# Relative-position products that hold a 64×48 corner of the array for each head, in place of 128×48

## The chip, the cores and the metric

The kernel runs on one core of one Trainium2 chip. The metric is the device time of one execution, in microseconds (us). Three runs of the kernel before gave 2831.45, 2834.18 and 2834.56 us, a median of 2834.18. Cores work with five engines: TensorE (PE in the profile) multiplies matrices, and its weight loads have a row of their own (PEld); VectorE is DVE, ScalarE is ACT, GpSimd is POOL, and SyncE (SP) issues most DMAs.

## The reference

Two layers run on an image of 48 × 48 positions (2304 tokens) with 768 channels. The first is a transformer block with 12 heads of 64 channels, and the second a block of Fourier transforms and small matrix products. The change lies in the attention of the first:

```python
attn = jnp.einsum('bqc,bkc->bqk', q * scale, k)
coords = jnp.arange(H)[:, None] - jnp.arange(H)[None, :] + (H - 1)
Rh = rel_pos_h[coords]
Rw = rel_pos_w[coords]
r_q = q.reshape(B * nh, H, W, hd)
rel_h = jnp.einsum('bhwc,hkc->bhwk', r_q, Rh)
rel_w = jnp.einsum('bhwc,wkc->bhwk', r_q, Rw)
attn = (attn.reshape(B * nh, H, W, H, W) + rel_h[:, :, :, :, None] + rel_w[:, :, :, None, :]).reshape(B * nh, H * W, H * W)
attn = jax.nn.softmax(attn, axis=-1)
out = jnp.einsum('bqk,bkc->bqc', attn, v)
```

For every query at row h and column w, `rel_h` is its product with 48 vectors that depend on h, and `rel_w` with 48 vectors that depend on w. Both are small products: 64 channels, 48 vectors, and the 48 queries that share an h or a w.

## The kernel before

**Heads.** Channels lie on partitions. Two heads make a pair: `qT` holds head 0 on partitions 0 to 63 and head 1 on 64 to 127, for all 2304 tokens. `pr` counts the six pairs. A chunk `c` is G = 384 queries, eight image rows; each pair has six.

**A chunk.** For each of 18 key tiles `kt`, `scores` (L684) makes scores of both heads in one PSUM tile `sp`. `content` (L670) multiplies 64 channels of keys with 64 of queries, one head on each half of the rows of the array. `position` (L679) adds the relative terms in a single fp32r instruction per head, from `terms` and a constant `select`. ACT takes the exponential (L689) into `main`. Then come 18 `products` with the values (L702), in six groups of three key tiles; each product contracts over 128 keys and gives 64 channels, head 0 on PSUM partitions 0 to 63 and head 1 on 64 to 127. DVE sums the exponentials for the denominators (L833).

**The relative products.** `relT` (L213) has partitions, head j, direction (0 for h, 1 for w), and 112 vectors. For j = 0 the vectors are on partitions 0 to 63 and zeros on 64 to 127; for j = 1 the other way about (`constants`, L319). So one matmul with all 128 partitions of `qT` gives the products of one head alone. `relative(pr, c)` (L288, matmul L296) makes eight rows of `rel_h`, and `columns(pr, i)` (L264, matmul L272) eight columns of `rel_w`. Each is a batch of 8 × 2 matmuls into one PSUM bank, head j at partition 64 j. The moving operand has 48 columns. For `pr` = 0, `columns` reads `qT` and writes PSUM with strides; later pairs read `by_column`, a copy in order that ACT makes (L694). Each fp32 matmul is two instructions in the profile, each with its weight load, so a batch shows 32 matmuls. After a batch, `two_parts` (L233) copies the bank twice on ACT (L240, L241) and subtracts on DVE (L242); DMAs then spread the rows into `terms`.

**The order.** The order of PE's work is the order of the code: the attention runs under a manual schedule for PE and SP, and in its loop for ACT and DVE as well. `between` (L785) hangs the small work before the six groups of products. In chunks 0 to 2 of a pair, `relative` for three chunks later goes ahead of group 0. In chunk 3 of all but the last pair, three `columns` for the next pair go ahead of groups 0, 1 and 2; in chunk 4 again three, and a `relative` ahead of group 3; in chunk 5 a `relative` ahead of groups 0 and 2. Group 0 follows the scores directly, the others follow products. Nine batches of pair 0 run earlier, in the last third of the query, key and value projections (L642 to L648), whose matmuls (L529, L561) use 128 rows and 128 columns of the array. `inverses` (L731) puts a 128×48 matmul with 32 moving columns ahead of group 4 of each chunk.

After the attention come the projection (L918), the MLP (L1291, L1351, L1355) and the second layer (L1383 to L1639).

Of the kernel before, what the change touches and what calls it, by code (L numbers as in the profile page):

```python
# [20 lines left out]
HW = 48  # L21
# [25 lines left out]
def block_then_afno(  # L47
# [147 lines left out]
    with ExitStack() as flag_scope:  # L195
# [12 lines left out]
        with ExitStack() as att:  # L208
# [4 lines left out]
            relT = cst.tile([P, 2, 2, 112], F32, name="relT")  # L213
# [13 lines left out]
            def small_bank():  # L227
                banks.append(banks.pop(0))
                return banks[-1]
# [3 lines left out]
            def two_parts(hi, lo, src):  # L233

                both = shared[:, ds(3 * T + (copies[0] % 2) * G, G)]
                copies[0] += 1
                dims = {f"x{i}": k for i, k in enumerate(src.shape[1:])}
                names = " ".join(dims)
                both = both.rearrange(f"p ({names}) -> p {names}", **dims)
                nc.scalar.copy(both, src)  # L240
                nc.scalar.copy(hi, src)  # L241
                nc.vector.tensor_tensor(lo, both, hi.bitcast(F32), ALU.subtract)  # L242
# [19 lines left out]
            by_column = None  # L262

            def columns(pr, i):  # L264

                qT = heads[pr][0].rearrange("p (c b h w) -> p b w c h", c=6, b=3, h=8)
                bank = small_bank()
                ps = bank.rearrange("p (w c h) -> p w c h", w=8, h=8)
                for r in range(8):
                    w = 8 * i + r  # L270
                    for j in range(2):
                        nc.tensor.matmul(  # L272
                            bank[ds(64 * j, HW), ts(r, HW)] if pr else ps[ds(64 * j, HW), r],
                            relT[:, j, 1, 47 - w : 95 - w],
                            by_column[:, w] if pr else qT[:, w // 16, w % 16],
                            start=True, stop=True,
                        )
                hi, lo = (
                    a.rearrange("p (c b h w) -> p b w c h", c=6, b=3, h=8)[
                        :, i // 2, ds(8 * (i % 2), 8)  # L280
                    ]
                    for a in (col_hi, col_lo)
                )
                two_parts(hi, lo, ps)
# [3 lines left out]
            def relative(pr, c):  # L288

                qT = heads[pr][0][:, ts(c, G)].rearrange("p (b h w) -> p h b w", b=3, h=8)  # L290
                hp = small_bank()
                ps = hp.rearrange("p (b h w) -> p h b w", b=3, h=8)
                for r in range(8):
                    h = 8 * c + r
                    for j in range(2):
                        nc.tensor.matmul(  # L296
                            ps[ds(64 * j, HW), r], relT[:, j, 0, 47 - h : 95 - h], qT[:, r],
                            start=True, stop=True,
                        )
                row_hi = r_pool.tile([P, G], F32R, name="row_hi")  # L300
                row_lo = r_pool.tile([P, G], F32R, name="row_lo")
                two_parts(row_hi, row_lo, hp)
                terms = b_pool.tile([P, 3, 3, G], F32R, name="terms")
                ready[pr, c] = terms
                for j in range(2):
                    for n, (row, column) in enumerate(((row_hi, col_hi), (row_lo, col_lo))):
                        for i in range(3):
                            rows = ds(64 * j + 16 * i, 16)
                            nc.sync.dma_start(
                                out=terms[ds(64 * j + 16 * n, 16), i].bitcast(F32),  # L310
                                in_=row[rows].bitcast(F32).unsqueeze(1).to_broadcast([16, 3, G]),
                            )
                            nc.sync.dma_start(
                                out=terms[ds(64 * j + 32 + 16 * n, 16), :, i].bitcast(F32),
                                in_=column[rows, ts(c, G)].bitcast(F32)
                                .unsqueeze(1).to_broadcast([16, 3, G]),
                            )
# [12 lines left out]
            def queries_keys_values(qkv):  # L330
# [263 lines left out]
                for p in range(T // TB):  # L594
# [13 lines left out]
                    for n, (kind, i) in enumerate(orders[p]):  # L608
# [33 lines left out]
                        if p == 2 and n == 0:  # L642
                            fetch(0)
                        elif p == 2 and n in (1, 2, 3):
                            for j in (0, 1):
                                columns(0, 2 * (n - 1) + j)
                        elif p == 2 and n in (4, 6, 8):
                            relative(0, n // 2 - 2)  # L648
                        elif p == 2 and n == 5:
                            fetch_values(0)  # L650
                    part_by_part.close()

            with tc.manual_schedule(engines={mybir.EngineType.PE, mybir.EngineType.SP}):
# [8 lines left out]
                by_column = o_pool.tile([P, HW, HW], F32, name="by_column", bufs=1)  # L662
# [122 lines left out]
                def between(pr, c, acc):  # L785

                    last = pr == NC - 1
                    work = {
                        1: [partial(denominators, pr, c, acc)],
                        4: [partial(inverses, pr, c)],  # L790
                        5: [partial(left_apart, pr, c), stored],
                    }
                    if last and c > 2:
                        work[5] += [partial(spread_out, 0), partial(scaled, 1), stored]
                    else:
                        work[5] += [partial(spread_out, 1), partial(scaled, 1)]
                    if c < 3:
                        work[0] = [partial(relative, pr, c + 3)]
                    elif not last and c < 5:
                        for n in range(3):  # L800
                            work.setdefault(n, []).append(partial(columns, pr + 1, 3 * (c - 3) + n))
                        if c == 4:
                            work[3] = [partial(relative, pr + 1, 0)]
                    elif not last:
                        work[0] = [partial(relative, pr + 1, 1)]
                        work[2] = [partial(relative, pr + 1, 2)]
                    if not last and c in (2, 3):
                        for n in range(3):
                            i = 3 * (c - 2) + n
                            work.setdefault(n + (1, 3)[c - 2], []).append(  # L810
                                partial(in_columns, pr + 1, i)
                            )
                    return work
# [192 lines left out]
        with tc.If(safe < 1):  # L1006
            with ExitStack() as att:
# [18 lines left out]
                relT = cst.tile([HD, 2, 112], F32, name="g_relT")  # L1026
# [8 lines left out]
                for pr in range(NC):  # L1035
                    w3 = []
                    for n, name in enumerate(("g_wq", "g_wk", "g_wv")):
                        w = w_pool.tile([P, NC, P], F32, name=name)
# [36 lines left out]
                    for sg in range(T // SG):  # L1075
# [20 lines left out]
                        for i in range(2):  # L1096
                            hp = psum.tile([P, G], F32, name="g_hp", tag="m")
                            for r in range(8):
                                h = sg * 16 + i * 8 + r
# [13 lines left out]
                        for i in range(2):  # L1113
                            wp = psum.tile([P, 24, 16], F32, name="g_wp", tag="m")
                            for r in range(24):
                                w = i * 24 + r
# [712 lines left out]
```

## Time and profile before

| what | value |
|---|---|
| median of three runs | 2834.18 us |
| the profiled execution, its own time | 2834.65 us |
| its span, first to last instruction | 2832.9 us |
| mean granted TensorE clock | 0.996 of full |
| from first scores to start of the last chunk | 403.06 to 1388.31 us |
| matmuls at L272, by array shape | 1152 of 128×48 |
| matmuls at L296, by array shape | 1152 of 128×48 |
| matmuls at L670 and L679, by array shape | 2592 and 1296 of 64×128 |
| matmuls at L702, by array shape | 2592 of 128×64 |

How to read it: a line of a group names the line of code, the engine, the operation, what it writes and reads, then the rows × columns of the array that a matmul holds ("128*48"), the shape and type of what moves, and the count. Behind the bar are busy time in us, the mean duration of one in ns, and the idle time ahead of it. A line of the timeline begins with its start and its length in us; consecutive instructions of one kind are merged, with their count. A matmul's duration is a latency with a modelled end, and matmuls overlap; the distance from start to start tells how fast they follow each other.

### The profile page before, as it was taken

The numbers are of one execution on the slowest core, as the hardware profiler recorded it, in microseconds if no ns is written. First come the engines' busy times: TensorE is split into PE (matmuls) and PEld (weight loads), VectorE is DVE, ScalarE is ACT, GpSimd is POOL, SyncE is SP. The second block draws the span as 40 slices with busy tenths as digits, with TensorE's granted clock in tenths as the row PEclk, the third lists the DMA queues.
The fourth block names the chain that finished last, engine by engine and source line by source line (L and its number), as shares of the span: only waits on it lengthen the run. The fifth ranks groups of instructions, "written<-read, shape, count | busy, mean of one in ns | idle before, by whom it ended". The sixth has DMA issues, their size and how long they took to land. (4 is left out here: it accounts for less than half of the span.)

```text
span 2832.9 us, 41042 instructions
## 1 busy us (share of the span) xinstructions
PE 2788.5 (98%) x15759; PEld 1716.2 (61%) x15759; DVE 1700.6 (60%) x2520; ACT 920.6 (32%) x1466; POOL 668.7 (24%) x662
## 2 busy tenths in 40 slices
PE   8999999999999999999999999999999999999998
PEld 4555655656656565665555555555555555556887
DVE  5434236767676767676756756565565566566665
ACT  1101135656566565665401201131101201102332
POOL 2505010000000000000164233342242422222432
PEclk9999999999999999999999999999999999999999
DMA  4535375273664737455332112131121212123254
GB/s 149 182 103 162 106 158 111 58 133 69 105 126 65 132 64 133 85 82 99 110 132 79 53 65 67 45 101 56 45 67 62 95 45 67 45 70 108 62 162 142
DMA packets 218430, 269.09 MB, mean 95 GB/s; under 512 B 24645, under 2 KB 197053, under 8 KB 216689
## 3 DMA queue, kind: packets, MB, share of 16 engines
q1 hardware_dynamic: 215720, 264.33, 37.5%
q8 instruction: 127, 2.08, 0.3%
q10 hardware_dynamic: 2440, 1.84, 0.2%
q14 instruction: 79, 0.64, 0.1%
q0 software_dynamic: 64, 0.20, 0.0%
HBM read 150.25 MB, written 52.32 MB: 72 GB/s over the span
## 5 line engine op out<-in xcount | busy, mean ns | idle before, releaser
L689 ACT ACTIVATE main<-sp 128x768 f32<-128x768 f32 x648 | 516.3, 812 | 34.5 <-PE sp L679 19.6
L833 DVE TENSOR_TENSOR pairs<-pairs,main 128x1536 f32<-128x1536 f32 x252 | 443.0, 1758 | 27.1 <-DVE pairs L833 0.9
L679 PE MATMUL sp<-terms,select 64*128 64x384 f32 x1296 | 412.0, 629 | 0.0
L1353 DVE TENSOR_TENSOR main<-o,main 128x384 f32<-128x384 f32 x540 | 298.7, 556 | 39.3 <-PE o L1351 1.2
L1291 PE MATMUL h<-shared,w 128*128 128x384 f32 x864 | 296.6, 486 | 0.7 <-POOL w2s L167 0.7
L670 PE MATMUL sp<-shared 64*128 64x384 f32 x1296 | 265.2, 485 | 1.6 <-ACT row_hi L241 1.0
L670 PE MATMUL sp<-qT,kT 64*128 64x384 f32 x1296 | 264.1, 484 | 0.0
L1291 PEld LDWEIGHTS h<-shared,w 128*128 128x128 f32 x864 | 163.9, 190 | 116.1 <-POOL w2s L167 1.3
L735 POOL TENSOR_TENSOR inverse<-inverse,rden 24x32 f32<-24x32 f32 x36 | 15.1, 421 | 926.5 <-DVE sums L734 887.5
L1291 PE MATMUL h<-shared,w1s 128*128 128x384 f32 x648 | 226.6, 486 | 0.0
L1297 ACT ACTIVATE hT<-c,vec 128x384 f32<-128x384 f32 x108 | 66.5, 615 | 465.1 <-DVE c L1303 465.0
L702 PE MATMUL op<-main,shared 128*64 128x384 f32 x1296 | 217.4, 488 | 0.0
L702 PE MATMUL op<-main,v 128*64 128x384 f32 x1296 | 216.4, 488 | 0.0
L833 DVE TENSOR_TENSOR pairs<-main 128x1536 f32<-128x1536 f32 x36 | 63.3, 1758 | 248.1 <-ACT main L689 248.1
L1303 DVE TENSOR_TENSOR c<-h,u 128x384 f32<-128x384 f32 x108 | 60.1, 557 | 212.4 <-PE h L1291 212.4
L1351 PE MATMUL o<-w,hT 128*128 128x384 f32 x432 | 174.8, 487 | 2.4 <-DVE mv L125 2.0
L1351 PE MATMUL o<-w2s,hs 128*128 128x384 f32 x432 | 174.9, 487 | 1.6 <-DVE hs L162 1.6
L679 PEld LDWEIGHTS sp<-terms,select 64*128 64x128 f32 x1296 | 125.3, 186 | 83.7
L1291 PEld LDWEIGHTS h<-shared,w1s 128*128 128x128 f32 x648 | 123.1, 190 | 85.8
L167 POOL TENSOR_TENSOR w2s<-w 128x384 f32<-128x384 f32 x36 | 35.9, 998 | 566.0 <-DMA w<-in_mlp_w_dram 424.0
L529 PE MATMUL m<-main 128*128 128x384 f32 x504 | 164.6, 488 | 2.4 <-DVE main L179 1.8
L702 PEld LDWEIGHTS op<-main,v 128*64 128x64 f32 x1296 | 96.9, 137 | 92.7 <-issue 67.7
(209 smaller groups left out, 4136.6 us busy)
## 6 DMA issues: line engine op xcount, KB each, us to landing
w<-in_mlp_w_dram SPq DMA_DIRECT2D x72, 768.0 KB
terms<-col_parts SPq DMA_DIRECT2D x432, 72.0 KB
terms<-row_hi SPq DMA_DIRECT2D x216, 72.0 KB
terms<-row_lo SPq DMA_DIRECT2D x216, 72.0 KB
main<-in_qkv_w_dram SPq DMA_DIRECT2D x36, 384.0 KB
z<-zt SPq DMA_DIRECT2D x48, 192.0 KB
x<-in_x_blocks_dram SPq DMA_DIRECT2D x18, 384.0 KB
k_d<-o SPq DMA_DIRECT2D x36, 192.0 KB
```

Source lines behind the costliest of these rows:

```text
L167: eng.tensor_tensor(t[0], b12, b11, ALU.subtract)
L529: nc.tensor.matmul(bank, a[:, c, :], b[:, c, :], start=(first and c == 0), stop=(c == 2), skip_group_check=not first,)
L670: nc.tensor.matmul(sp[:, j, :G], kT[at, ts(kt, P)], qT[at, ts(c, G)], start=first, stop=not first,)
L679: nc.tensor.matmul(sp[:, j, :G], select[at, a % 2], ready[pr, c][at, a // 2, b], start=first, stop=not first,)
L689: nc.scalar.activation(p, sp[:, :, :G], AF.Exp, scale=HD**-0.5)
L702: nc.tensor.matmul(op[ts(j, 64)], v[:, kt, ts(j, 64)], exps[:, kt, j, :], start=(kt == 0), stop=(kt == NT - 1),)
L833: nc.vector.tensor_tensor(pairs, so_far, exps[:, ds(kt - 1, 2)], ALU.add)
L1291: nc.tensor.matmul(bank[i], a[:, c, :], b[:, c, :], start=(start and c == 0), stop=(c == 2), skip_group_check=not start,)
L1297: nc.scalar.activation(h[:, i, ts(k, G)], src, AF.Gelu, bias=col(V_B1 + 2 * n + i))
L1303: nc.vector.tensor_tensor(t, src, other, ALU.add)
L1351: nc.tensor.matmul(bank[k], a, b, start=start, stop=True, skip_group_check=not start)
L1353: nc.vector.tensor_tensor(dst, bank[k], dst, ALU.add)
```

## The change

Both the stationary and the moving operand of the two small matmuls are cut to the 64 partitions of their head. Head 0 then reads partitions 0 to 63 and writes PSUM partitions 0 to 63; head 1 reads and writes 64 to 127. The counts of instructions, the 48 moving columns, PSUM banks, order, copies and DMAs are as before. The zeros in `relT` stay and are not read.

```diff
@@ columns
                         nc.tensor.matmul(
                             bank[ds(64 * j, HW), ts(r, HW)] if pr else ps[ds(64 * j, HW), r],
-                            relT[:, j, 1, 47 - w : 95 - w],
-                            by_column[:, w] if pr else qT[:, w // 16, w % 16],
+                            relT[ts(j, 64), j, 1, 47 - w : 95 - w],
+                            (by_column[:, w] if pr else qT[:, w // 16, w % 16])[ts(j, 64)],
                             start=True, stop=True,
                         )
@@ relative
                         nc.tensor.matmul(
-                            ps[ds(64 * j, HW), r], relT[:, j, 0, 47 - h : 95 - h], qT[:, r],
+                            ps[ds(64 * j, HW), r], relT[ts(j, 64), j, 0, 47 - h : 95 - h],
+                            qT[ts(j, 64), r],
                             start=True, stop=True,
                         )
```

## The prediction

> **What bounds the kernel now.** I read the page first, then the groups of TensorE instructions, then stretches of the timeline around the changed matmuls.
>
> ```profile
> span 2832.9 us, 41042 instructions
> PE 2788.5 (98%) x15759; PEld 1716.2 (61%) x15759; DVE 1700.6 (60%) x2520; ACT 920.6 (32%) x1466; POOL 668.7 (24%) x662
> ```
>
> TensorE (PE) is busy for 98% of the span. A modelled busy time alone proves little, so I asked for the busy time by stretch. The attention lies between the first scores and the start of the last chunk:
>
> ```profile
> 403.06:1388.31 985.25, 984.63 (x8386) 591.50 (x8386) 660.62 (x557) 606.34 (x821) 56.52 (x69) 1.00 0.53 97
> ```
>
> The columns are span, then PE, PEld, DVE, ACT and POOL. PE leaves 0.6 us of 985 empty, at full clock; ACT and DVE are busy for about two thirds. Whatever lengthens or shortens PE's own sequence here moves the end by as much. The groups of PE that matter:
>
> ```profile
> L670 PE MATMUL sp<-qT,kT 64*128 64x384 f32 x1296 | 264.1, 484 | 0.0
> ...
> L702 PE MATMUL op<-main,v 128*64 128x384 f32 x1296 | 216.4, 488 | 0.0
> ...
> L272 PE MATMUL small<-by_column,relT 128*48 128x48 f32 x960 | 27.0, 209 | 0.0
> ...
> L296 PE MATMUL small<-qT,relT 128*48 128x48 f32 x576 | 16.4, 210 | 0.0
> ```
>
> "128*48" is the part of the array that an instruction holds: rows, then columns. An fp32 matmul appears twice, so a batch of 8 positions and 2 heads has 32 instructions. There are 72 batches (36 at L272, 36 at L296). Scores run at 64*128, the products with the values at 128*64, and the changed matmuls at 128*48. Means are no help (209 ns is a pipelined latency); spacing of starts is. In the timeline (start, duration, ...), a batch between two groups of products:
>
> ```profile
> 503.91 0.49 PE L702 MATMUL op<-main,shared 128*64 128x384 f32 x2
> 504.24 0.89 PE L272 MATMUL small<-by_column,relT 128*48 128x48 f32 x32
> 504.95 0.83 PE L702 MATMUL op<-main,shared 128*64 128x384 f32 x4
> ```
>
> A pair of products (one per head) normally repeats after 0.322 us, and here the batch follows after 0.33: no seam. The batch takes 0.71 us, 16 pairs at 45 ns; the single starts (the trace's records, to the ns) show the two heads of a pair 7 ns apart. So both heads already run side by side. 384 columns in 322 ns make 0.84 ns a column, 40 ns for 48: the pair is within 5 ns of one stream's time. Now the same batch inside 128*128 work (first line: one instruction of 0.322 us), and the seam from scores to products where no batch lies:
>
> ```profile
> 343.83 0.49 PE L529 MATMUL m<-main 128*128 128x384 f32 x1
> 344.24 0.93 PE L296 MATMUL small<-shared,relT 128*48 128x48 f32 x32
> 345.10 0.59 PE L529 MATMUL m<-main 128*128 128x384 f32 x1
> ```
>
> ```profile
> 1348.26 0.63 PE L679 MATMUL sp<-terms,select 64*128 64x384 f32 x2
> 1348.73 0.81 PE L670 MATMUL sp<-qT,kT 64*128 64x384 f32 x4
> 1349.08 0.63 PE L679 MATMUL sp<-terms,select 64*128 64x384 f32 x2
> 1349.64 0.87 PE L702 MATMUL op<-main,v 128*64 128x384 f32 x4
> ```
>
> 343.83 to 344.24 is 0.415 by the single starts (343.829, 344.244), 93 ns more than the 322 the instruction needs. L679 to the next L670 is 0.47; L679 to L702 is 0.56, again about 95 ns more. Every place in this trace where the shape changes has this gap, and none where it stays. Behind the gap the first weight load is uncovered too: the first two pairs of L702 there start 0.373 apart, not 0.322 (1349.643, 1350.016).
>
> **What the Trainium skill says.** "TensorEngine Tiling (Array Packing)", Key Properties: changing the tiling mode, not only the tile, drains the TensorE; 128×64 and 64×64 are different modes. The trace agrees for the changes it has, 93 to 97 ns each (the sums use 94), and shows that 48 columns count with 64. "TensorE: Matmul & The Clock Gate", Part 3 (The mechanism): a weight load overlaps matmuls in flight only when the row groups differ. That would favour the change, but the trace does not agree: the loads at L272 (125 ns each) are spaced like their matmuls, and share all rows. "PSUM — Partial Sum Buffer", PSUM bank collisions: by one quoted statement different row tiles cannot access the same bank at once, while what was measured there is a collision within one bank and 32-partition quarter. The changed pair shares a bank but not partitions; no row of before shows such a pair, since scores put each head in its own bank.
>
> **The change, part by part.**
>
> *Instructions.* None is added or removed: 2304 here, each with 48 moving columns. No DMA, copy or semaphore moves. What SBUF reads is halved, but spacing is set by columns: 64-row scores need 322 ns a pair, 128-row products also 322. I take zero for the spacing. Bounds: down to 40 ns, gaining 5 ns on 1008 attention pairs, 5.0 us; up to serial heads, +40 ns a pair (rival D).
>
> *Mode seams.* A batch goes from 128*48 to 64*48. In the attention it no longer has the products' mode. The other 9 batches, six at L272 and three at L296, lie in the projection stage. Of the 63 in the attention, 33 follow directly on scores and 30 on products; all 63 are followed by products. Counting: c 0 to 2 have one batch each (18, after scores); c 3 has three (one after scores), c 4 four (one), c 5 two (one), for five head pairs.
> - After scores: the entry was a change (64×128 to 128×64) and stays one (64×128 to 64×64): 0. Its exit becomes one: 63 exits in all.
> - After products: the entry becomes one: 30.
> - The 9 early batches: before and after are 128×128 work (one meets the scores), a change on both sides then and now: 0.
>
> 93 new changes. An exit costs 94 ns plus the weight load no longer covered: first to second pair of products 0.373 after a change, 0.339 behind a batch now (502.284, 502.623), so 34; 128 ns. An entry costs 94 plus 80 against 43 ns from first to second small pair (501.528, 501.608; 504.235, 504.278), 37; 131 ns.
> 63 × 0.128 + 30 × 0.131 = 8.1 + 3.9 = **12.0 us**.
>
> What is not shown: a change of the row split alone (128×64 to 64×64), which all 93 are. Bounds: 0, if only column splits drain, and 131 ns. I take the full price, because the skill names the mode as a whole and because 64×128 to 128×64, changing both, costs 95, the same as a column change alone: one drain, not a sum. Below nothing is excluded, as the seam now has no gap.
>
> *What hides it.* Nothing: PE has no slack in this stretch. Behind each seam wait only PE's own next matmuls, then the copies at L240 and L241, whose terms are used three chunks later or, for columns, a chunk later. ACT and DVE get some room; neither sets the end.
>
> *Sum.* The profiled execution took 2834.65 us (span 2832.9 and 1.75 around it), 0.5 above the median of 2834.18. Its 12.0 us go on the median: **2846.2**.
>
> **The rivals.**
> - **A, all new changes drain** (forecast): 2846.2. With the weight loads covered, 93 × 0.094 = 8.7, 2843; at half the price of a change, 2840; with 3 ns more spacing, 2850 or so. 2840 to 2851. Chance 0.73.
> - **B, a row split alone doesn't drain**: no seam is added, the spacing is the same: 2834, 2832 to 2838. For it: no such change is in the trace. Against: every other change pays alike. In effect the change then does nothing. Chance 0.13.
> - **C, faster**: reading one half of the partitions for each head frees the stream. Place: the spacing of pairs. 1008 pairs from 45 to 40 save 5.0 us; the 96 strided pairs of the first columns, now about 87 ns (two batches take 2.87 us from 294.45 to the next product at 297.32, a gap of some 0.1 included), to 40 save 4.5: 9.5 in all, 2825, if changes are free. It decides by 0.2% (5.7 us) only if a change costs under (9.5 − 5.7) / 93 = 41 ns; at full price it ends at 2837. Against: rows don't set spacing at L670 and L702. Chance 0.06.
> - **D, the corners run one after the other**, over the shared bank or the weight loads: 40 ns on 1152 pairs, 46 us, and 12.0 for seams: 2892. For it: the bank statement, and no such pair in the trace. Against: 64-row heads at L670 run side by side. Chance 0.08.
>
> **How the numbers follow.** The measurement of this kernel can tell about 0.2% from no change, 5.7 us: slower begins at 2839.9, faster ends at 2828.5. A and D make slower 0.79 (the lower edge of A, 0.02, goes to same); B with that and the part of C that is cancelled make same 0.16; C leaves faster 0.05. Leaving out C and D costs 0.14, so the range is A with B: 2832 to 2851.
>
> **What would show it.** In the changed trace: L702 to L272 0.41 instead of 0.33, last small pair to products 0.13 instead of 0.04, both in 0.32 to 0.37 for the following pair; chunk lengths up by 0.13 (c 0 to 2), 0.65 (c 3), 0.91 (c 4) and 0.39 (c 5); spacing within a batch still 45 ns; stretches outside the attention unchanged. Seams without gaps mean B; pairs under 45 ns speak for C, at 80 ns or more for D. The forecast is wrong if row-only changes are cheap or spacing moves by over 5 ns.

## The result, and the profile after

The changed kernel takes 2844.21 us (median of six runs, 2841.64 to 2844.98); six runs of the kernel before gave a median of 2832.69. The ratio is 1.0038, with a 95% interval of 1.0025 to 1.0051: 11.5 us slower. The forecast was 12.0 us more, 2846.2.

The page of the profiled execution (2844.98 us) does not show a cause. A gap between two starts that lies inside the modelled length of the matmul ahead of it counts as busy time:

```profile
span 2843.2 us, 41042 instructions
...
PE 2799.1 (98%) x15759; PEld 1720.3 (61%) x15759; DVE 1701.2 (60%) x2520; ACT 919.5 (32%) x1466; POOL 670.7 (24%) x662
```

The counts of instructions are the same, and PE is busy 10.6 us longer. Cut by stretch, from the first scores to the start of the last chunk, and from there to the end (span, then PE, PEld, DVE, ACT, POOL):

```profile
400.56:1398.17 997.61, 996.99 (x8387) 594.11 (x8387) 660.27 (x557) 605.92 (x821) 56.54 (x69) 1.00 0.52 95
1398.17:2843.20 1445.03, 1415.36 (x5915) 894.62 (x5913) 888.68 (x1711) 257.92 (x544) 498.93 (x501) 0.99 0.25 80
```

The attention went from 985.25 to 997.61: 12.36 us more. The rest behind it is 0.4 longer, and the first scores come 2.5 earlier, which together give the 10.3 us of the two spans. Most of the 2.5 has nothing to do with the change: the 101st matmul of the execution, long before any relative product, already began 1.9 us earlier (41.95 against 43.88).

The groups have the new shape, and the rest of their lines is nearly unchanged:

```profile
L272 PE MATMUL small<-by_column,relT 64*48 64x48 f32 x960 | 27.7, 208 | 0.0
L296 PE MATMUL small<-shared,relT 64*48 64x48 f32 x576 | 16.6, 208 | 0.0
L296 PE MATMUL small<-qT,relT 64*48 64x48 f32 x576 | 16.6, 208 | 0.0
L272 PE MATMUL small<-shared,relT 64*48 64x48 f32 x192 | 8.6, 258 | 0.0
```

A group's busy time shows little of the seams, the places where the shape changes. The timeline shows them. The same batch as before between two groups of products:

```profile
504.53 0.81 PE L703 MATMUL op<-main,shared 128*64 128x384 f32 x4
505.28 0.92 PE L272 MATMUL small<-by_column,relT 64*48 64x48 f32 x32
506.13 0.54 PE L703 MATMUL op<-main,shared 128*64 128x384 f32 x2
```

By the single starts, the batch held its place for 0.72 us before (504.235 to 504.953), and now for 0.85. The last pair of products (504.855) is followed after 0.422 us in place of 0.322, well inside its modelled length of 0.49. Within the batch, pairs still follow each other at 45 ns (505.402, 505.447, 505.492), the two heads 7 ns apart. From the last small pair (505.987) to products it is 142 ns, not 45; and the first two pairs of products stand 373 ns apart, not 338. All 63 batches of the attention are left in this way, and the 30 among products are entered in this way, to within 2 ns. Among 128×128 work, where a batch changed the shape before as well, the picture is the old one (the first line is one instruction, which needs 0.322 us before the next of its kind can start):

```profile
341.73 0.49 PE L530 MATMUL m<-main 128*128 128x384 f32 x1
342.15 0.92 PE L296 MATMUL small<-shared,relT 64*48 64x48 f32 x32
343.00 0.59 PE L530 MATMUL m<-main 128*128 128x384 f32 x1
```

0.42 us in and 0.85 to the end of the batch, as against 0.41 and 0.86 before.

### The profile page after: what moved, and what is told of

The parts are those of the page before. It is cut to its first block, busy times and chain, and to the rows that moved or that the text cites. A ratio compares the mean times of both kernels' runs of the same rounds, so it can differ in the third digit from the quotient of the medians.

```text
span 2843.2 us, 41042 instructions
## 1 busy us (share of the span) xinstructions
PE 2799.1 (98%) x15759; PEld 1720.3 (61%) x15759; DVE 1701.2 (60%) x2520; ACT 919.5 (32%) x1466; POOL 670.7 (24%) x662
```

## The experiments

The theory at the start: each side of a batch at which the row split of the array is new costs 0.13 to 0.14 us, and a batch in itself costs what it did. The first rival: each cut batch is slower in itself, 12.4 us over 63 batches, wherever it stands. Further rivals: the price belongs to these products alone (their operands, or a PSUM bank shared by two row halves), or to any stationary operand that fills fewer rows than its neighbours. In what follows "attention" is the stretch from the first scores to the start of the last chunk, which is steadier than the whole time: 985.25 us before, and within 0.06 of that in the two versions that were expected to add nothing. Each such figure is from one profiled execution.

**Only the batches among products (30).**

```diff
-                            relT[:, j, 1, 47 - w : 95 - w],
+                            relT[at, j, 1, 47 - w : 95 - w],
...
+                        at = ts(j, 64) if pr and i % 3 else slice(None)
...
+                        at = ts(j, 64) if pr and c in (0, 2) else slice(None)
```

> The kernel before, with the row cut in only those 30 attention batches that follow products (columns 1 and 2 of each three, and the relative batches of chunks 0 and 2 of pairs 1 to 5). Theory (each new change of the array's shape costs 0.13 to 0.14 us): 30 entries and 30 exits, 30 x 0.137 + 30 x 0.131 = 8.0 us over before; chunks 0 to 2 and the last three as before, chunk 3 +0.54, chunk 4 +0.80, chunk 5 +0.27. Rival (a cut batch is slower in itself, the 12.4 us of the changed kernel's attention spread over 63 batches, 0.197 each): 5.9 us, and each of the three chunk kinds in proportion to its batches (0.39, 0.59, 0.20).

Measured: ratio 1.0033 (1.0021 to 1.0045), 9.5 us. Its attention, in the columns of the stretches above:

```profile
401.58:1394.90 993.32, 992.71 (x8387) 591.59 (x8387) 660.27 (x557) 606.27 (x821) 56.58 (x69) 1.00 0.53 96
```

8.07 us more, against 8.0 and 5.9. By chunk, from first scores to next first scores, chunks 3, 4 and 5 are 0.54, 0.81 and 0.27 longer, the others not at all. One chunk holds both shapes side by side:

```profile
499.47 0.64 PE L682 MATMUL sp<-terms,select 64*128 64x384 f32 x2
500.04 0.93 PE L273 MATMUL small<-by_column,relT 128*48 128x48 f32 x32
500.80 2.12 PE L705 MATMUL op<-main,shared 128*64 128x384 f32 x12
502.85 0.92 PE L273 MATMUL small<-by_column,relT 64*48 64x48 f32 x32
503.70 2.16 PE L705 MATMUL op<-main,shared 128*64 128x384 f32 x12
```

The twelve instructions of products take 2.05 us before the cut batch (500.80 to 502.85; 1.95 in the kernel before, 502.284 to 504.235). The uncut batch leaves after 0.76, the cut one after 0.85.

**Only the batches directly after scores (33).** The same edit, with `pr and i % 3 == 0` and `c > 2 or pr and c == 1`.

> The kernel before, with the row cut in only those 33 attention batches that follow scores directly. Theory: the entry is a change of shape already, so 33 exits alone, 33 x 0.131 = 4.3 us over before; 0.13 in each of 33 chunks. Rival (0.197 us for each cut batch, wherever it lies): 6.5 us, more than the kernel with the other 30 batches cut.

Measured: ratio 1.0013 (1.0007 to 1.002), 4.1 us.

```profile
402.75:1392.28 989.53, 988.91 (x8387) 593.81 (x8387) 660.48 (x557) 606.26 (x821) 56.59 (x69) 1.00 0.53 96
```

4.28 us more, against 4.3 and 6.5, 0.13 in each of the 33 chunks. More batches cut, at half the price of the other 30. The rival of a price for each batch falls, and the two parts (8.07 and 4.28) add up to the whole (12.36).

**Only the nine early batches.** The same edit, with `not pr` and `not pr and c < 3`.

> The kernel before, with the row cut in only the nine early batches, among the 128x128 work of the projections. Theory: both sides of such a batch are a change of shape already: 0 us, with 0.41 into and 0.13 out of the batch as before; attention 985.25 us as before. Rival (0.197 us for each cut batch): 1.8 us, visible in the trace. A side question: the changed kernel reached its first scores 2.5 us earlier than before; if that comes from these nine batches, it shows here, and if it is scatter between executions it need not.

Measured: ratio 0.9995 (0.9986 to 1.0004).

```profile
402.15:1387.40 985.25, 984.63 (x8386) 591.50 (x8387) 660.49 (x557) 606.30 (x821) 56.59 (x69) 1.00 0.53 97
```

Nothing is added in the attention, but these nine batches lie ahead of it. In their own places nothing is added either: the first that lies between two 128×128 matmuls comes 0.416 us after the one ahead of it and holds its place for 0.852 (0.415 and 0.855 in the kernel before), and the strided ones are shorter, as told at the end. The first scores come at 402.15, inside the 401.58 to 403.06 of executions whose early batches were not cut. So most of the head start of the changed kernel's profile (400.56) is scatter, and some 0.2 us of it come from these batches.

**96 rows.** Head 0 reads partitions 0 to 95, so the operand is cut but not the row split:

```diff
+                        at = slice(0, 96) if j == 0 else slice(None)
```

> The kernel before, with head 0 of every small relative product cut to partitions 0 to 95, of which 64 to 95 hold zeros; head 1 as before. Theory: 96 rows hold the array in the same split as 128, so no seam appears: 0 within noise, pair spacing 45 ns, products to batch 0.32 to 0.33. Rival (any stationary operand that doesn't fill the rows of its neighbours drains the array): 93 changes, some 12 us, and also between the two heads of each pair, so far more.

Measured: ratio 0.9999 (0.9991 to 1.0007).

```profile
503.27 0.81 PE L705 MATMUL op<-main,shared 128*64 128x384 f32 x4
503.91 0.89 PE L273 MATMUL small<-by_column,relT 96*48 96x48 f32 x32
504.63 0.83 PE L705 MATMUL op<-main,shared 128*64 128x384 f32 x4
```

0.32 in (a pair at 503.59), 0.72 to the products: no seam (the merged line shows the shape of head 0). Attention 985.31. Fewer rows alone, 96 in place of 128 for one head, cost nothing and gain nothing.

**A different product, cut to 64 rows.**

```diff
-                    nc.tensor.matmul(den[:48, :32], part, gather, start=True, stop=True)
+                    nc.tensor.matmul(den[:48, :32], part[:64], gather[:64], start=True, stop=True)
```

> The kernel before, its relative products untouched; the small matmul of the denominators (between products, ahead of group 4 of each chunk) reads 64 of its 128 partitions, so half of each sum is left out. Theory: a change of the row split costs wherever it stands: an entry and an exit in each of 36 chunks, 0.137 + 0.131, and its two passes can no longer slip between the products, some 0.03 to 0.05 more: 0.27 to 0.32 a chunk, 9.6 to 11.5 us in all. Rival (the price belongs to the relative products, their operands or their PSUM bank shared by two row halves): 0 to 1 us.

Measured: ratio 1.0032 (1.002 to 1.0044), 8.8 us; attention 994.20, 8.95 more, 0.256 for each of its 35 chunks. The relative products are as they were, and the price is there. First a chunk of the kernel before, then one of this version:

```profile
1357.43 0.19 PE L731 MATMUL small<-gather,part 128*48 128x32 f32 x1
1357.44 0.54 PE L702 MATMUL op<-main,v 128*64 128x384 f32 x1
1357.46 0.21 PE L731 MATMUL small<-gather,part 128*48 128x32 f32 x1
1357.51 4.06 PE L702 MATMUL op<-main,v 128*64 128x384 f32 x23
```

```profile
447.32 7.92 PE L702 MATMUL op<-main,shared 128*64 128x384 f32 x48
455.17 0.27 PE L731 MATMUL small<-gather,part 64*48 64x32 f32 x2
455.37 4.09 PE L702 MATMUL op<-main,shared 128*64 128x384 f32 x24
```

Before, the two passes slip in between products; with 64 rows, the products stop for them. The rival that the price belongs to the relative products falls: this product is alone, with no second head beside it in its bank. The amount is a little under the 0.27 to 0.32 expected, and the single starts show what I had missed. Before, the two passes ran in head 0's half of the array, and pushed the heads of all later products of the chunk 47 ns apart, until the scores waited for the later one (1361.038 and 1361.085 in the kernel before). With the seam, both heads restart together and end 7 ns apart (458.972, 458.979). 0.256 plus these 0.040 is 0.296, which is within the expected range.

**The same cut, in another place.** In the changed kernel, 18 batches move from a place after scores to one among products; the control moves them in the kernel before.

```diff
-                        work[0] = [partial(relative, pr, c + 3)]
+                        work.setdefault(3, []).append(partial(relative, pr, c + 3))
```

> The changed kernel, with the relative batch of chunks 0 to 2 hung ahead of group 3 of the products, and no longer ahead of group 0 (18 batches). Theory: a batch directly after scores shares its entry with the seam that is there anyway; among products it needs one of its own: 18 x 0.137 = 2.5 us over the changed kernel, some 14.7 over before; chunks 0 to 2 at 27.80 in place of 27.67. Rival (a price for each cut batch): as the changed kernel, some 12 over before.

> The kernel before, with the same move of 18 batches. Theory: at 128x48 a batch has the products' shape, and a place among them costs what the other place does, within 0.01 us a batch by the chunk lengths: +0.2 us, no difference to measure. If the move itself costs (copies on ACT in another place, a bank that comes free later), it shows here as it does in the moved version of the changed kernel, and is to be taken off there.

Measured: the cut kernel moved has ratio 1.0047 (1.0031 to 1.0064), 13.9 us over before; the control 1.0002 (0.9994 to 1.0011). Attention, cut and control:

```profile
400.55:1400.92 1000.37, 999.75 (x8386) 592.16 (x8386) 663.43 (x557) 606.02 (x821) 56.52 (x69) 1.00 0.52 95
```

```profile
402.29:1387.79 985.50, 984.88 (x8387) 591.62 (x8387) 663.67 (x557) 606.30 (x821) 56.51 (x69) 1.00 0.52 97
```

The cut version is 2.76 over the changed kernel, less 0.25 for the move itself: 2.51, or 0.139 for each of 18 new entries, where 0.137 was expected.

**The cut batches between products and scores.**

```diff
-                        work[2] = [partial(relative, pr + 1, 2)]
+                        work[6] = [partial(relative, pr + 1, 2)]
...
                             finish(pr, c, op)
+                            for what in work.get(6, ()):
+                                what()
```

The third `columns` of chunk 3 and the `relative` of chunk 4 move to 6 in the same way.

> The changed kernel, with 15 of its 30 batches that lie among products (the third columns of chunk 3, the relative batch of chunk 4, the second of chunk 5) moved behind the last products of their chunk, so that scores follow. Theory: the way from products to scores is a change of shape anyway, so a batch there pays its entry alone and spares the exit: 15 x 0.131 = 2.0 us less than the changed kernel, attention 995.6 in place of 997.60, chunks 3, 4 and 5 each 0.13 shorter, and still some 10 us over before. Rival (a price for each cut batch, or the array must be emptied per batch whatever follows): as the changed kernel, 997.6.

Measured: ratio 1.0038 (1.0024 to 1.0053), 10.9 us over before.

```profile
513.44 0.81 PE L703 MATMUL op<-main,shared 128*64 128x384 f32 x3
514.17 0.92 PE L272 MATMUL small<-by_column,relT 64*48 64x48 f32 x32
515.03 0.92 PE L671 MATMUL sp<-shared 64*128 64x384 f32 x4
```

Attention 995.32: 2.29 less than the changed kernel, 0.153 for each batch, where 0.131 was expected. The direction tells the theories apart; the size shows a term that I had taken from the wrong place. 0.131 is what the exit of a cut batch costs more than that of an uncut one. A cut batch that leaves the products takes more with it: 0.422 us up to the batch, 0.852 that it holds and 0.373 behind it give way to two plain steps of 0.322, which is 1.003 less. Ahead of the scores it adds the 0.852 alone, since the step from the last product is 0.416 with and without it (513.758 to 514.174 here, 1361.085 to 1361.500 in the kernel before), and the first pair of scores stands 0.43 ahead of the second in both. The difference, 0.151, accounts for the 0.153. The same move in the kernel before was not run. The whole times cannot tell these 2 us: their intervals are wider.

## Why the prediction was right

The forecast (case A) held in its sign, place and size: 12.0 us forecast, 12.36 in the attention, 11.5 in the medians. That the medians come so close is in part chance, since their interval reaches from 7 to 14 us; the attention is the closer test.

- *No slack on PE in the attention*: right. All of the attention's growth arrives at the end of the span, apart from the scatter at the start.
- *Spacing of pairs, change taken at zero*: right. 45 ns before and after, and 84 ns for the strided pairs of the first columns, which took 84 to 87. So C (faster) and D (heads one after the other) both fall. Two row halves in one PSUM bank, on different partitions, run side by side: the starts show no trace of one waiting for the other.
- *63 exits of 0.128*: 0.131 measured (142 − 45, and 373 − 339). The batches after scores alone gave 4.28 / 33 = 0.130.
- *30 entries of 0.131*: this term was 6 ns too small. An entry costs 416 − 316 = 100 from the last product's second head, where I had put 94, and 80 − 43 = 37 for the weight load. The new shape starts 416 ns after the last start of the old one, behind products (504.861 to 505.277) as behind a single 128×128 matmul (0.415). The 94 is right counted from there; but the old step of 322 runs from first head to first head, and the second starts 6 to 7 ns later. 30 × 0.137 = 4.1, with 63 × 0.131 = 8.3: 12.4 in all.
- *Row split alone, the unknown*: the whole forecast stood on it, and the trace of before could not show it. It costs what a column split does. The 96-row kernel bounds it from the other side: fewer rows as such are free, and somewhere from 96 down to 64 the price sets in. What the Trainium skill says in "TensorEngine Tiling (Array Packing)" under Key Properties, that a change of the tiling mode drains TensorE, agrees with this for rows too, with 97 to 100 ns measured for the gap of one such change. The trace shows the gap; that the array is being emptied in it is the page's account.
- *"Every place in this trace where the shape changes has this gap"*: too wide. The sums do not use it, but it spoke against B. Three transposes of 128*12 and 128*1 among 128×128 matmuls (90.962, 212.978 and 1431.368 us in the kernel before) come 0.323 us after the matmul ahead of them, without a gap, and the next follows after 0.11. So the printed shape alone does not tell whether there will be a seam. Why these three are different was not tried.
- *Early batches, 0*: right, by the kernel that cuts them alone (0.2 us shorter, if anything).
- *Chunk lengths*: 0.13, 0.65, 0.91 and 0.39 forecast; 0.13, 0.67, 0.94 and 0.40 measured, by the entry term again.
- *B (row change free)*: falls with the seam at 505.28.

None of the versions with cut batches beats the kernel before. In the attention, every cut batch needs at least one change of shape that an uncut one does not, and gets nothing for it, since both heads ran side by side already in the two column halves.

## What to carry to other kernels

Before cutting a small matmul to its useful rows, look at how its neighbours on PE hold the array. In these runs 96 rows went with 128 and 64 did not; 48 columns went with 64 and not with 128. If the cut sets the matmul apart from its neighbours, each new seam costs some 0.13 us of PE time, against a whole batch of 0.72 here, and zeros that fill the rows may be the cheaper choice. That holds where, as here, the cut makes the matmuls themselves no faster. If a different shape is needed, put the batch where the shape changes anyway: there one seam is spared. To find the cost, compare starts across the seam; groups and busy shares show little of it.

## What the runs showed of the hardware that I had not expected

- A small matmul in one column half can set the two heads' streams 47 ns apart for the rest of a group, and a seam sets them together again: 0.040 us a chunk back, found in the denominators' kernel.
- The strided early batches (L272 for the first pair) became steadier when each head read its own half: fifteen steps took 1.25 to 1.26 us in all six, where they took 1.26 to 1.31 before, 0.2 us in all. The other traces divide in the same way: 1.25 to 1.26 where these batches are cut, 1.26 to 1.32 where they are not. The contiguous batches did not change. What makes the difference was not tried.
